# A selective state-space block beside a quantized feed-forward block on one core: six products of a step's second half go from VectorE to GpSimd, and the scan's result goes to SBUF

## The chip, the cores and the metric

The kernel runs on one core of one Trainium2 chip. The core has TensorE (PE in the profile, its weight loads PEld), VectorE (DVE), ScalarE (ACT), GpSimd (POOL) and SyncE (SP); each works through its own instructions in order, and here nearly all DMAs are issued from SP's queue. The metric is device time in microseconds for one launch. Before the change three runs took 5172.91, 5178.5 and 5181.34 us: the median is 5178.5 us.

## The reference

The input is x, 8 sequences of 1024 tokens with 512 channels. It is normalized over channels, and two blocks work on the result and are added to x:

```python
xn = _layernorm(x, axis=-1)
x = x + attn(xn) + ffn(xn)

# attn: D_INNER = 1024, D_STATE = 16
xz = xn @ W_in;  x_branch, z = split(xz, 2)
xc = silu(causal_depthwise_conv(x_branch, conv_w, 4 taps) + conv_b)
ssm = xc @ W_x;  B, C, dt = ssm[..., :16], ssm[..., 16:32], softplus(ssm[..., -1:] + dt_bias)
A = -exp(A_log)
h[t] = h[t-1] * exp(dt[t] * A) + (dt[t] * xc[t]) * B[t]     # per channel and state
y[t] = sum over states of h[t] * C[t]
out = ((y + xc * D_param) * silu(z)) @ W_out

# ffn: 512 -> 1408 -> 512; every operand is rounded blockwise to FP4 and back first
h = silu(q(xn) @ q(w_gate).T) * (q(xn) @ q(w_up).T)
out = q(h) @ q(w_down).T
```

The recurrence runs over 8 x 1024 tokens, 1024 channels and 16 states.

## The kernel before

**Steps and pairs.** The 8192 tokens are cut into 16 steps of T = 512, two steps to a sequence. A step's channels are 8 groups `j` of 128. The state-space part lays 32 channels times 4 states on the 128 partitions: a group `j` has 4 sets of 32 channels and 4 sets `q` of 4 states. Two sets of channels (`h` and `h + 1`) make one instruction of 2 x 512 columns, a *pair*. So a step has 8 x 4 x 2 = 64 pairs, numbered `k` = 0 to 63 in the order j, q, h, and the program 1024.

**What a pair does.** POOL makes `u` = (dt x) B (`make_u`, L638) in SBUF, from a pool with three buffers. ACT makes `ah` = exp(dt A) in PSUM, two instructions, two buffers (`make_a`, L650). In the second step of a sequence (odd steps) ACT also puts the carried state into one column of `u` (L656). In `scan`, DVE runs the recurrence over both halves in one instruction, `ah` times the running value plus `u`, and writes the states over `ah` (L668); in the first step of a sequence (even steps) it copies the last column into `state` (L673); then it multiplies the states by C into `hc` in SBUF (L675), from a pool with four buffers. PE sums over states with small matmuls (`sum_states`, L685) into `py`. After the last `q` of a group, DVE's `gate` (L703, L704) adds D x, multiplies by silu(z) and writes `y`, of which there is one buffer.

**Around the pairs.** `sweep` writes every engine's order out by hand. For pair g it issues `make_u` for pair g + 2, `make_a` for pair g + 1, then `scan` for pair g, then the work that `later` put off to this pair (`issue`), and then gives PE other work as long as a planned time per pair allows. That other work is, by place in the step: from pair 2 to 9 `finish`, the output matmul of the step before (`po`, L735); from pair 9 to 43 `ahead`, the projections for the next step (`px`, `pz`, L437 and L498), whose convolution runs on ACT and POOL (L454, L460); and in the rest the feed-forward matmuls. Steps 0 to 9 (SPLIT = 10) carry the gate and up matmuls with their quantization, which uses DVE, ACT and POOL; steps 10 to 15 carry the down matmul (`downs`, `pod`, L894), whose input `hTr` is loaded over SP's queue into two buffers (L883). DVE adds each result to the residual (`add`, L722). In step 15 there is no next step to project for.

**In a step's second half** `parameters` and `steps_of` prepare the next step. `parameters` is the matmul with W_x. `steps_of`, four times at a distance of three pairs, has ACT write softplus into two `dd` tiles (L577), then POOL multiply them by x (`rest`, L582) and SP store them (L584). There are two `dd` buffers, so ACT's next softplus waits until both stores have landed. SP's queue then holds the loads that follow in program order: `rep` (L593), B and C for the next step (L566), the gate's inputs (L696), `hTr` and the residual (L714).

Of the kernel before, what the change touches and what calls it, by code (L numbers as in the profile page):

```python
# [9 lines left out]
F32 = mybir.dt.float32  # L10
BF16 = mybir.dt.bfloat16
AF = mybir.ActivationFunctionType
ALU = mybir.AluOpType
# [4 lines left out]
P = 128  # L18
# [9 lines left out]
T = 512  # L28
SG = 4
D4 = P // SG  # L30
NQ = P // D4
NG = 4
FB = 256
SPLIT = 10
# [3 lines left out]
ENOUGH = 2.0  # L38
MOST = 6.0
AGAIN = "again"  # L40
TAIL = 12


# [134 lines left out]
class Net:  # L178
# [200 lines left out]
    def issue(self):  # L379
# [3 lines left out]
        while self.due.get(self.now):  # L383
            item = work, bank, key, act = self.due[self.now].pop(0)
            if key in [i[2] for i in kept] or (act and used >= ENOUGH and self.scanning):
                kept.append(item)
                continue
            if work() is AGAIN:
                kept.append(item)
# [103 lines left out]
    def project_z(self, s, j, w):  # L493
# [8 lines left out]
        def copy():  # L502
            if i == 0 and s.stored < h:
                return AGAIN
            if i == 0:
# [6 lines left out]
    def silus(self, s, h):  # L512
        nc = self.nc
        if s.convolved < 2 * (h + 1) or s.copied < 2 * (h + 1):
            return AGAIN
        xs, z = s.xc[:, 2 * h : 2 * h + 2, :], s.z[h]
# [117 lines left out]


    def make_u(self, s, j, q, h):
        u = self.pool.tile([P, 2, T], F32, tag="u", name=f"u_{s.c}_{j}_{q}_{h}", bufs=3)
        self.nc.gpsimd.tensor_tensor(  # L638
            u, s.reps[j][:, h : h + 2, 1, :], s.B[q].unsqueeze(1).to_broadcast([P, 2, T]), ALU.mult
        )  # L640
        self.us.append(u)
# [20 lines left out]
    def scan(self, s, j, q, h):  # L662

        nc = self.nc
        ah, u = self.ahs.pop(0), self.us.pop(0)
        g = j * NQ + h
        a = ah.rearrange("p i t -> p (i t)")
        nc.vector.tensor_tensor_scan(  # L668
            a, a, u.rearrange("p i t -> p (i t)"),
            0.0 if s.first else self.state[:, g, q : q + 1], ALU.mult, ALU.add,  # L670
        )
        if not s.last:
            nc.vector.tensor_copy(self.state[:, g : g + 2, q], ah[:, :, T - 1])  # L673
        hc = self.pool.tile([P, 2, T], F32, tag="hc", name=f"hc_{s.c}_{j}_{q}_{h}", bufs=4)
        nc.vector.tensor_tensor(hc, ah, s.C[q].unsqueeze(1).to_broadcast([P, 2, T]), ALU.mult)  # L675
        s.hcs.append(hc)

    def sum_states(self, s, j, q):

# [268 lines left out]
    def sweep(self, pairs, now, others, cost):  # L948
# [5 lines left out]
        left = cost + len(now) // per * (29.0 + 64.0 + sums)  # L954
        slots = len(now) - TAIL
        credit = 0.0
# [146 lines left out]
```

## Time and profile before

| | |
|---|---|
| median of three runs | 5178.5 us |
| the profiled execution | 5171.58 us, span 5169.7 us |
| mean granted TensorE clock | 0.916 |
| busy: PE, DVE, ACT, POOL | 4357.2, 4463.7, 3368.9, 4050.4 us (84, 86, 65, 78%) |
| steps 0 to 9 (460 to 3590 us): PE, DVE, POOL | 2720, 2688, 2603 of 3130 us |
| steps 10 to 14 (3591 to 4884 us) | 254 to 263 us a step |
| step 15 and the end | 286 us |

A profile line of the page's fifth part names line, engine and operation, then output<-inputs with shapes and the count; behind the bar stand the busy time in us, the mean of one in ns, and the engine's idle time just before these instructions with what ended it. In a table of stages each column is an engine's busy time in that stretch with its instruction count. A line of waits says who waited for whom, the total in us, how often, and the longest. The chain is followed back from the last instruction; a piece gives its start, its length and its work.

### The profile page before, as it was taken

Reading aid. Unit: us, or ns where it says so; the run is one execution under the profiler, and the core shown is the slowest. Engines: PE = TensorE matmul, PEld = TensorE weight load, DVE = VectorE, ACT = ScalarE, POOL = GpSimd, SP = SyncE. Lnnn points to the kernel's source line nnn. Section 1 sums busy time; section 2 is a strip of 40 time slices with the busy share of each in tenths; the row PEclk is TensorE's granted clock in tenths of the full one; section 3 lists DMA queues with packets and bytes.
Section 4 is the critical chain, followed back from the end, with each engine's and each line's share of the span. In section 5 each row is a group of like instructions: output and inputs, shape, how many; then the busy total and the mean of one; then the engine's idle time right before and its main releaser. Section 6 shows DMA issues by size and latency. Waiting matters only on the chain. (4 is left out here: it accounts for less than half of the span.)

```text
span 5169.7 us, 52154 instructions
## 1 busy us (share of the span) xinstructions
PE 4357.2 (84%) x16324; PEld 2286.0 (44%) x16324; DVE 4463.7 (86%) x4087; ACT 3368.9 (65%) x5037; POOL 4050.4 (78%) x2302
## 2 busy tenths in 40 slices
PE   5535889888898898989898898986999999999975
PEld 2324555554555556455554555551333333333321
DVE  6756888888888988888887898888999999999997
ACT  5655766767667677775767867676656665656543
POOL 5887888878888888887887888887768676767664
PEclk9656999999899999999999999996999999999986
DMA  6665566575656657566575656757686868686852
GB/s 196 198 205 157 143 185 182 155 199 170 180 165 173 192 165 208 143 188 180 162 201 154 191 166 182 200 145 207 178 229 177 239 182 240 175 236 184 228 132 61
DMA packets 582275, 937.45 MB, mean 181 GB/s; under 512 B 53216, under 2 KB 329696, under 8 KB 579824
## 3 DMA queue, kind: packets, MB, share of 16 engines
q1 hardware_dynamic: 571600, 931.61, 64.3%
q10 hardware_dynamic: 10400, 2.52, 0.2%
q8 instruction: 130, 2.13, 0.2%
q14 instruction: 145, 1.19, 0.1%
HBM read 676.76 MB, written 257.20 MB: 181 GB/s over the span
## 5 line engine op out<-in xcount | busy, mean ns | idle before, releaser
L638 POOL TENSOR_TENSOR u<-rep,B 128x1024 f32<-128x1024 f32 x1024 | 2411.3, 2361 | 760.9 <-DVE ah L668 691.6
L650 ACT ACTIVATE ah<-rep,A 128x512 f32<-128x512 f32 x2048 | 1415.8, 692 | 1129.0 <-DVE hc L675 1090.3
L675 DVE TENSOR_TENSOR hc<-ah,C 128x1024 f32<-128x1024 f32 x1024 | 1249.5, 1220 | 77.3 <-PE py L685 35.1
L668 DVE TENSOR_TENSOR_SCAN ah<-ah,state,u 128x1024 f32<-128x1024 f32 x512 | 1199.5, 2343 | 87.0 <-ACT u L656 85.9
L668 DVE TENSOR_TENSOR_SCAN ah<-ah,u 128x1024 f32<-128x1024 f32 x512 | 1169.3, 2284 | 52.3 <-ACT ah L650 46.0
L685 PE MATMUL py<-hc,summed 128*32 128x512 f32 x4096 | 653.5, 635 | 170.9 <-DVE hc L675 119.0
L771 PE MATMUL pu<-wu,xq 128*128 128x256 f32 (+1 forms) x3072 | 693.9, 383 | 101.9 <-ACT hT L824 63.1
L771 PE MATMUL pg<-wg,xq 128*128 128x256 f32 (+1 forms) x3072 | 661.7, 373 | 69.8 <-ACT hT L824 23.3
L771 PEld LDWEIGHTS pu<-wu,xq 128*128 128x128 f32 x3072 | 571.7, 203 | 250.6 <-ACT hT L824 86.7
L894 PE MATMUL pod<-dT,hTr 128*128 128x512 f32 x1408 | 641.7, 606 | 13.3 <-DMA hTr<-hT 9.6
L771 PEld LDWEIGHTS pg<-wg,xq 128*128 128x128 f32 x3072 | 554.0, 195 | 210.3 <-issue 69.5
L498 PE MATMUL pz<-xT,wz 128*128 128x512 f32 x1024 | 506.3, 641 | 69.5 <-ACT h L782 34.8
L437 PE MATMUL px<-xT,wx 128*128 128x512 f32 x1024 | 491.9, 625 | 38.8 <-ACT h L782 21.4
L735 PE MATMUL po<-Wout,y 128*128 128x512 f32 x1024 | 463.8, 604 | 10.7 <-ACT hT L824 4.4
L460 POOL TENSOR_TENSOR xc<-xc,taps 128x509 f32<-128x509 f32 x360 | 413.7, 1149 | 44.3 <-ACT taps L454 25.5
L894 PEld LDWEIGHTS pod<-dT,hTr 128*128 128x128 f32 x1408 | 262.7, 192 | 395.2 <-issue 365.1
L498 PEld LDWEIGHTS pz<-xT,wz 128*128 128x128 f32 x1024 | 204.1, 205 | 338.9 <-issue 232.3
L685 PEld LDWEIGHTS py<-hc,summed 128*32 128x32 f32 x4096 | 91.8, 110 | 564.7 <-DVE hc L675 278.7
L437 PEld LDWEIGHTS px<-xT,wx 128*128 128x128 f32 x1024 | 195.3, 198 | 317.7 <-issue 224.2
L735 PEld LDWEIGHTS po<-Wout,y 128*128 128x128 f32 x1024 | 191.2, 192 | 278.7 <-issue 258.4
L786 DVE TENSOR_TENSOR h<-h,pu 128x512 f32<-128x512 f32 x192 | 121.9, 638 | 179.4 <-PE pu L771 166.3
L650 ACT ACT_TABLE_LOAD x209 | 268.1, 1283 | 3.7
(125 smaller groups left out, 4538.4 us busy)
## 6 DMA issues: line engine op xcount, KB each, us to landing
rep<-ddd SPq DMA_DIRECT2D x512, 512.0 KB, 7.1
ddd<-dd SPq DMA_DIRECT2D x128, 512.0 KB, 3.5
hTr<-hT SPq DMA_DIRECT2D x64, 704.0 KB, 5.8
wg<-gu SPq DMA_DIRECT2D x80, 512.0 KB, 4.9
wu<-gu SPq DMA_DIRECT2D x80, 512.0 KB, 5.9
hT<-hT SPq DMA_DIRECT2D x80, 512.0 KB, 2.9
wx<-in_L_attn_W_in_dram SPq DMA_DIRECT2D x128, 256.0 KB, 3.0
wz<-in_L_attn_W_in_dram SPq DMA_DIRECT2D x128, 256.0 KB, 2.9
```

The lines of the kernel that those rows point to most:

```text
L437: nc.tensor.matmul(px, w[:, k, :], s.xT[:, k, :], start=(k == 0), stop=(k == self.KM - 1))
L460: tt(ca[:, H0 - k :], ca[:, H0 - k :], taps[k][:, : T - H0 + k], ALU.add)
L498: nc.tensor.matmul(b[0], w[:, k, :], s.xT[:, k, :], start=(k == 0), stop=(k == self.KM - 1))
L638: self.nc.gpsimd.tensor_tensor(u, s.reps[j][:, h : h + 2, 1, :], s.B[q].unsqueeze(1).to_broadcast([P, 2, T]), ALU.mult)
L650: nc.scalar.activation(ah[:, i, :], s.reps[j][:, h + i, 0, :], AF.Exp, scale=self.A[:, g, q : q + 1])
L668: nc.vector.tensor_tensor_scan(a, a, u.rearrange("p i t -> p (i t)"), 0.0 if s.first else self.state[:, g, q : q + 1], ALU.mult, ALU.add,)
L675: nc.vector.tensor_tensor(hc, ah, s.C[q].unsqueeze(1).to_broadcast([P, 2, T]), ALU.mult)
L685: nc.tensor.matmul(s.py[i * D4 : (i + 1) * D4, :], self.summed, hcs[i // 2][:, i % 2, :], start=(q == 0), stop=(q == NG - 1),)
L735: nc.tensor.matmul(b[0], s.y[:, j, i * P : (i + 1) * P], self.Wout[:, j, :], start=(j == 0), stop=(j == self.J - 1),)
L771: nc.tensor.matmul(b[0][:, i, :], xq[pair][:, k, i * P : (i + 1) * P], w[:, k, :], start=(k == 0), stop=(k == self.KM - 1),)
L786: nc.vector.tensor_tensor(rows, rows, b[0], ALU.mult)
L894: nc.tensor.matmul(b[0], h[:, k, :], dT[:, k, :], start=(k == 0), stop=(k == self.KF - 1))
```

## The change

For six pairs of every step from step 10 on, k = 42, 46, 50, 54, 58 and 62 (all with `h` = 0), the scan writes its states over `u` in SBUF instead of over `ah` in PSUM. For these pairs POOL instead of DVE copies the last column into `state` (even steps) and multiplies the states by C into `hc`. `ah` is then free when the scan ends, and the `u` buffer when POOL's product ends. The pool of `u` has four buffers instead of three, in all steps. POOL's new instructions stand in its queue where `scan` is issued, so behind `u` of pair k + 2 and ahead of what `issue` gives POOL at that pair and of `u` of pair k + 3.

```diff
+ASIDE = (42, 46, 50, 54, 58, 62)
...
     def make_u(self, s, j, q, h):
-        u = self.pool.tile([P, 2, T], F32, tag="u", name=f"u_{s.c}_{j}_{q}_{h}", bufs=3)
+        u = self.pool.tile([P, 2, T], F32, tag="u", name=f"u_{s.c}_{j}_{q}_{h}", bufs=4)
...
         a = ah.rearrange("p i t -> p (i t)")
+        uf = u.rearrange("p i t -> p (i t)")
+        aside = s.c >= SPLIT and (j * NG + q) * NQ // 2 + h // 2 in ASIDE
+        to = u if aside else ah
         nc.vector.tensor_tensor_scan(
-            a, a, u.rearrange("p i t -> p (i t)"),
+            uf if aside else a, a, uf,
             0.0 if s.first else self.state[:, g, q : q + 1], ALU.mult, ALU.add,
         )
+        hc = self.pool.tile([P, 2, T], F32, tag="hc", name=f"hc_{s.c}_{j}_{q}_{h}", bufs=4)
+        s.hcs.append(hc)
+        C = s.C[q].unsqueeze(1).to_broadcast([P, 2, T])
+        if aside:
+            if not s.last:
+                nc.gpsimd.tensor_copy(self.state[:, g : g + 2, q], to[:, :, T - 1])
+            nc.gpsimd.tensor_tensor(hc, to, C, ALU.mult)
+            return
         if not s.last:
-            nc.vector.tensor_copy(self.state[:, g : g + 2, q], ah[:, :, T - 1])
-        hc = self.pool.tile([P, 2, T], F32, tag="hc", name=f"hc_{s.c}_{j}_{q}_{h}", bufs=4)
-        nc.vector.tensor_tensor(hc, ah, s.C[q].unsqueeze(1).to_broadcast([P, 2, T]), ALU.mult)
-        s.hcs.append(hc)
+            nc.vector.tensor_copy(self.state[:, g : g + 2, q], to[:, :, T - 1])
+        nc.vector.tensor_tensor(hc, to, C, ALU.mult)
```

## The prediction

> **What bounds the kernel now.** I read the profiled execution in this order: the shares of the chain that ended last, busy time by stage, who waits for whom in the stages that are edited, and the chain piece by piece there. From the page, the chain's shares and two groups:
>
> ```profile
> DVE ah L668 11%; DVE hc L675 5%; PE po L735 4%; PE pod L894 3%; ACT ah L650 1%; PE py L685 1%; DMA xz<-z 1%; PE pz L498 0%; DMA hTr<-hT 0%; DMA rep<-ddd 0%; POOL u L638 0%; PE pu L771 0%; DVE py L703 0%; DVE r_True L722 0%; ACT taps L454 0%
> ...
> L638 POOL TENSOR_TENSOR u<-rep,B 128x1024 f32<-128x1024 f32 x1024 | 2411.3, 2361 | 760.9 <-DVE ah L668 691.6
> ...
> L675 DVE TENSOR_TENSOR hc<-ah,C 128x1024 f32<-128x1024 f32 x1024 | 1249.5, 1220 | 77.3 <-PE py L685 35.1
> ```
>
> The operation that moves, `hc`, costs 1.22 us on DVE; POOL's nearest row, `u`, with the same shapes and kinds of operand, costs 2.36 us. POOL idles 692 us before its `u`, waiting for a scan to give a buffer back. The chain is DVE, but with PE in it. Busy time by stage, for the first 42 pairs and the rest of steps 14 and 15 (columns: PE, weight loads, DVE, ACT, POOL, granted clock, DMA):
>
> ```profile
> 4629.90:4798.70 168.80, 163.56 (x470) 60.81 (x471) 160.88 (x148) 100.48 (x147) 128.25 (x75) 0.98 0.71 192
> 4798.70:4884.00 85.30, 83.89 (x253) 30.44 (x251) 83.88 (x78) 46.69 (x66) 60.48 (x30) 1.00 0.90 253
> 4884.00:5053.90 169.90, 131.30 (x368) 42.64 (x366) 161.64 (x109) 75.18 (x143) 100.22 (x43) 0.84 0.57 143
> 5053.90:5134.00 80.10, 38.46 (x92) 3.90 (x92) 78.27 (x48) 35.37 (x68) 44.67 (x19) 0.50 0.25 59
> ```
>
> In the second half of step 14, the edited part, DVE and PE are both busy 98% at a granted clock of 1.00. In step 15 the down matmul is over and PE is half idle: there DVE alone sets the time. So what PE waits for matters in steps 10 to 14. PE's waits in the second halves of step 10 (two lines) and of step 14:
>
> ```profile
> PE pod L894 <- DMA hTr<-hT: 4.1, 2, 3.2
> PE py L685 <- DVE hc L675: 0.8, 1, 0.8
> ...
> PE py L685 <- DVE hc L675: 1.4, 1, 1.4
> ```
>
> Steps 11, 12 and 13 have 1.9, 2.0 and 1.5 us. All five together are 4.9 + 1.9 + 2.0 + 1.5 + 1.4 = 11.7 us, and PE can be shortened there by no more. At the start of the next step DVE waits for PE (start of step 15; steps 11 to 14 show the second line with 0.7 to 0.8 us):
>
> ```profile
> DVE r_True L722 <- PE po L735: 3.8, 3, 3.4
> DVE y L704 <- PE po L735: 0.7, 1, 0.7
> ```
>
> `y` has one buffer, so the first gate of a step, about pair 9, waits until PE has finished the step before. A lead that DVE gains and PE does not is given back there. The chain in step 14 shows two more links:
>
> ```profile
> 4834.22 1.28 POOL dd L582
> ...
> 4835.52 8.01 DMA ddd<-dd
> ...
> 4843.60 1.21 ACT L577
> ...
> 4849.06 2.31 DVE ah L668
> ...
> 4852.73 1.05 PE py L685 x4
> 4853.79 9.64 PE pod L894 x22
> ```
>
> POOL's `dd` product is stored; the store must land before ACT may write the next `dd`; ACT stands before the next `ah`, and DVE waits for that. From 4852.73 on, PE runs without a gap into step 15.
>
> **The change, part by part.**
>
> *Removed from DVE.* 36 `hc` (six steps, six pairs) and 18 state copies (the even steps). The copy, 0.16 us, overlaps the end of the scan and the start of `hc`, so what goes is the distance between two scans. In step 15, around pairs 51 to 53:
>
> ```profile
> 5087.38 2.35 DVE L668 TENSOR_TENSOR_SCAN ah<-ah,state,u 128x1024 f32<-128x1024 f32 x1
> 5089.76 1.23 DVE L675 TENSOR_TENSOR hc<-ah,C 128x1024 f32<-128x1024 f32 x1
> 5090.90 2.35 DVE L668 TENSOR_TENSOR_SCAN ah<-ah,state,u 128x1024 f32<-128x1024 f32 x1
> ```
>
> From start to start it is 3.52 us, of which 2.35 is scan: about 1.17 us saved a pair, 36 x 1.17 = 42 us if nothing else held.
>
> *The scan that writes SBUF.* No scan does so in this trace. The nearest rows of 512 columns (L786 0.64, L704 0.69 into SBUF, L703 0.75 into PSUM) differ by 0.11 us, so the bound is plus or minus 0.11 x 36 = 4 us; I take 0, as the recurrence, not the destination, sets 2.29 us for 1024 columns against 1.22 of a plain product.
>
> *Added to POOL.* 36 products of 2.36 us (bounds 2.36 by `u`, 2.54 by two `dd` of 1.27) and 18 copies of about 0.19 (L464): 88 us, 14 to 15 in a half where POOL has 25 us idle. Each new product waits for its scan, and behind it stand the `u` three pairs on (2.5 + 2.4 = 4.9 us after the scan's end, wanted 7.1 after: covered) and the `dd` products, then SP's stores of `dd` and all loads queued on SP behind them. The order of PE, ACT and SP is unchanged.
>
> A rule that speaks against such a move: the Trainium skill, Trace Analysis, section on optimizing Scalar and DVE operations, says that POOL and DVE share an SBUF read port, so that shifting work between them may not help. The row against it: `hc` with one input in PSUM, one in SBUF and its output in SBUF, which the edited scan will be like, takes 1.214 to 1.227 us 1024 times, whatever POOL runs. By the rule the sum would lose what I price below; by the row it loses 0.
>
> *Step 15.* ACT has the next `ah` ready 0.5 us before the scan ends, `u` over 4 us, and PE waits. Six pairs of 1.17: -7.0 us, all on the path.
>
> *Steps 10 to 14*, by the time at which PE's last stretch begins:
> - Step 10: POOL runs the second pair of `dd` behind the product of pair 50, not before it. They ended at 3799.4; now scan 50 ends about 3797.7 (1.75 earlier), then 0.2 + 2.4 + 2.5 gives 3802.8, 3.4 later. SP's `hTr` load behind that store was issued at 3801.2 and PE waited 3.2 us for it; it goes 3.4 later, and 0.4 to 0.9 of the later `hTr` wait absorbs a part: +3.0.
> - Step 11: PE's 1.9 us wait for the gate at pair 58. DVE comes there with 1.17 of pair 42, little of 46 (ACT's softplus makes the next `ah` late), part of 50: -1.75.
> - Step 12: both waits for `hc`, 1.3 us, go and part of the `hTr` wait of 0.7: -1.7.
> - Step 13: the wait of 1.5 us goes if the store of the third `dd` pair lands in the usual 3.7 us (-1.5); it took over 8, and POOL issues it about 0.7 later (+0.7). Middle: -0.4.
> - Step 14: POOL's `dd` of the chain above ends at scan 50's end + 0.2 + 2.4 + 2.4 + 2.5. That scan ends 2.4 earlier, but a product and a copy more stand ahead of it: 0.1 later than before. With the same 8 us of landing nothing is gained; with 3.7, 1.4. I take -0.6.
>
> Sum -1.5 us; the bounds are -11.7 (all PE waits gone) and +12 (3 in four of the five).
>
> *The fourth `u` buffer* serves all sixteen steps. It lets POOL start one pair earlier where it now waits for a scan, 292 us in steps 0 to 9. But what other engines wait for POOL there, and POOL itself could have begun after such a wait, is small: DVE waited for `u` 3.9 us in all, ACT 11.7, PE's transposes for the last quantizing product 33, most of them with POOL busy up to that point. Bounds 0 and -18; I take -2.5.
>
> **Sum.** -7.0 - 1.5 - 2.5 = -11.0 us. The profiled execution took 5171.6 us (span 5169.7 and 1.9 around it), 6.9 below the median of the three runs, 5178.5; by it 5160.6, by the median 5167.5.
>
> **Rivals.**
> 1. *DVE alone is the bound* (for: its shares; against: 98% PE and its 11.7 us of waits). All 42 us come: 5136.
> 2. *Slower: the `dd` stores hold SP.* If in every step the second pair of `dd` falls behind a product as in step 10, `hTr` loads come 3.4 us late, and the softplus after them too. For: SP waited 32 us for `dd` products around the second half of step 10, and DMA is at 0.90. Against: in steps 11 to 14 `hTr` is mostly issued 9 to 14 us before use and lands in about 5.8. It decides once a `dd` ends over 4 us late: 5 x 3.4 = 17, less 7: 5188.5.
> 3. *The buffer is worth its upper bound* of 18: 7.0 + 1.5 + 18 = 26.5, 5152. For: POOL's 292 us; against: nobody waits long for it.
> 4. *POOL and DVE block each other.* Half a POOL product, 1.2 us, per edited scan is 43, less 11: 5210. Only the rule speaks for it.
> 5. *The change does nothing*: with PE bound to the end, 5178. Step 15, with PE half idle, speaks against it.
>
> **How the numbers follow.** The forecast has 0.60, and its own range, from its bounds, is 5157 to 5178; half of that lies beyond 0.2% (10.4 us, about what a measurement of this kernel can tell from no change), half within. Rival 1 has 0.06, 2 has 0.18, 3 has 0.12, 4 has 0.02, 5 has 0.02. Faster: 0.30 + 0.06 + 0.12 = 0.48; same: 0.30 + 0.02 = 0.32; slower: 0.18 + 0.02 = 0.20. Leaving out rival 1 and part of 3 below, and 4 and part of 2 above, gives 5150 to 5187.
>
> **What would show it.** Right: scans at the edited pairs of step 15 start 2.4 us after the one before and its second half is 7 us shorter; PE's waits in the second halves of steps 11 and 12 vanish and step 10's wait for `hTr` grows to over 6; DVE's wait for `po` at pairs 3 to 9 grows by what DVE gained. Wrong: second halves of steps 10 to 14 that are 5 us shorter without longer waits at the next step's start (rival 1), PE waits for `hTr` in every step (2), steps 0 to 9 shorter by over 10 us (3), or edited scans over 2.5 us (4).

## The result: 0.2% faster, and the profile after

Twenty runs of each kernel beside one another: 5163.82 us after (5153.99 to 5180.17), 5175.34 before (5161.43 to 5188.0). The ratio is 0.998, with a 95% interval of 0.9972 to 0.9988: 10.4 us faster (6 to 14.5). The predicted sum was 11.0.

The profiled execution has a span of 5171.4 us, longer than the 5169.7 of before. Its steps 0 to 9, where only a buffer was added, happen to end 12.2 us later (step 10 starts at 3603.1, before at 3590.9); steps 10 to 15, where the work moved, take 1568.3 us instead of 1578.8. Executions of one kernel spread over 26 us, so single profiles are read here only by stage, and a stretch of five steps is not known better than to some 7 us (e1 below, whose time is that of before, has 1282.5 us where before has 1289.9).

From the page after the change, the shares of the chain and the group of `u`:

```profile
PE pod L904 7%; DVE ah L672 6%; PE po L745 4%; DVE hc L686 3%; PE py L695 2%; ACT ah L651 1%; DMA xz<-z 1%; DMA hTr<-hT 1%; PE pz L499 1%; PE ps L538 1%; DMA rep<-ddd 1%; POOL u L639 1%; PE px L438 1%; POOL xc L461 1%; PE pu L781 0%
...
L639 POOL TENSOR_TENSOR u<-rep,B 128x1024 f32<-128x1024 f32 x1024 | 2402.2, 2362 | 380.4 <-DVE ah L672 262.1
```

The down matmul, 3% of the chain before, leads it now; the scan went from 11% to 6%. POOL's wait for a scan to give a `u` buffer back fell from 692 to 262 us. The instructions on `u` (count, then shortest, median and longest in ns):

```profile
L672 DVE TENSOR_TENSOR_SCAN ah<-ah,u x494: 2233/2289/2299, 463.6 to 4886.7; 128x1024 f32<-128x1024 f32 x165
L672 DVE TENSOR_TENSOR_SCAN ah<-ah,state,u x494: 2257/2350/2359, 795.5 to 5132.9; 128x1024 f32<-128x1024 f32 x165
L682 POOL TENSOR_TENSOR hc<-u,C x36: 2338/2354/2391, 3781.4 to 5133.1; 128x1024 f32<-128x1024 f32 x36
L672 DVE TENSOR_TENSOR_SCAN u<-ah,u x18: 2278/2278/2283, 3778.9 to 4883.4; 128x1024 f32<-128x1024 f32 x18
L681 POOL COPY state<-u x18: 186/188/194, 3781.3 to 4885.8; 128x2 f32<-128x2 f32 x18
L672 DVE TENSOR_TENSOR_SCAN u<-ah,state,u x18: 2340/2340/2345, 4045.5 to 5130.7; 128x1024 f32<-128x1024 f32 x18
```

The edited scans take 10 ns less than the others, and POOL's product 2.35 us. The busy times by stage, for both parts of steps 14 and 15 (columns: PE, weight loads, DVE, ACT, POOL, granted clock, DMA):

```profile
4640.10:4807.30 167.20, 162.05 (x473) 60.46 (x472) 160.98 (x149) 100.62 (x147) 130.49 (x76) 0.99 0.73 197
4807.30:4890.20 82.90, 80.55 (x243) 29.14 (x242) 76.09 (x66) 46.63 (x66) 73.13 (x41) 1.00 0.88 245
4890.20:5063.00 172.80, 133.94 (x377) 43.63 (x375) 161.70 (x109) 75.16 (x143) 101.57 (x44) 0.84 0.58 148
5063.00:5171.40 108.40, 64.23 (x160) 16.68 (x160) 76.26 (x49) 35.26 (x68) 57.91 (x25) 0.64 0.22 58
```

The second half of step 14 was 85.3 us with VectorE busy for 83.88; now it is 82.9 with 76.09. VectorE has lost 7.8 us of work and the stage 2.4. The second half of step 15 with the end of the program went from 115.8 to 108.4, where VectorE lost 7.5: everything arrived. This is the list of VectorE's instructions around pair 51 of step 15 (start, duration):

```profile
5090.34 2.34 DVE L672 TENSOR_TENSOR_SCAN u<-ah,state,u 128x1024 f32<-128x1024 f32 x1
5092.60 2.33 DVE L672 TENSOR_TENSOR_SCAN ah<-ah,state,u 128x1024 f32<-128x1024 f32 x1
5094.96 1.23 DVE L686 TENSOR_TENSOR hc<-ah,C 128x1024 f32<-128x1024 f32 x1
```

From the edited scan to the next it is 2.26 us; with a product between it is 3.50 here and was 3.52 before. An edited pair saves 1.26 us, not the 1.17 of the prediction: the next scan begins 0.08 us before the recorded end of this one.

Measured from pair 10 of a step (behind the point where VectorE waits for the end of the step before) to pair 10 of the next, in us:

| | step 10 | 11 | 12 | 13 | 14 | sum 10 to 14 | step 15 to the end |
|---|---|---|---|---|---|---|---|
| before | 260.3 | 259.3 | 255.1 | 260.1 | 255.1 | 1289.9 | 238.8 |
| after | 264.5 | 254.6 | 256.4 | 255.6 | 255.3 | 1286.2 | 231.7 |

In these five steps 30 x 1.26 = 38 us of VectorE's time went, and 3.6 of it came out (the sums are made of unrounded starts); traces of one kernel can differ by more than that here. The first table of waits shows who holds VectorE in this stretch, first before, then after the change (total us, times, longest):

```profile
DVE ah L668 <- ACT u L656: 12.1, 13, 2.8
DVE r_True L722 <- PE po L735: 11.6, 13, 3.4
DVE ah L668 <- ACT ah L650: 11.1, 4, 4.9
DVE r_False L722 <- DMA r_False<-in_L_attn_x_dram: 7.0, 2, 6.4
DVE y L704 <- PE po L735: 3.8, 5, 0.8
DVE r_True L722 <- DMA r_True<-rd: 1.9, 1, 1.9
```

```profile
DVE ah L672 <- ACT u L657: 20.2, 16, 3.3
DVE r_False L732 <- DMA r_False<-in_L_attn_x_dram: 13.7, 4, 7.6
DVE ah L672 <- ACT ah L651: 11.7, 4, 5.1
DVE r_True L732 <- DMA r_True<-rd: 11.3, 6, 5.6
DVE ah L672 <- POOL dd L583: 10.2, 2, 5.8
DVE r_True L732 <- PE po L745: 7.3, 10, 4.2
DVE r_False L732 <- DMA C<-ssm_d: 3.9, 1, 3.9
```

The prediction had VectorE's lead given back to PE (`po`). That wait fell from 11.6 to 7.3. What grew is the wait for residuals that `add` needs (7.0 + 1.9 before, 13.7 + 11.3 after, and the 3.9 of the last line, which is an `add` too) and the wait for a late `ah` or for the column of `u` that ACT fills. The line that names POOL's `dd` belongs there too: in step 14 that `dd` had ended 12 us before the scan, and ACT's `ah` came last. All lines of the scan together went from 23.2 to 42.1 us.

### The profile page after: what moved, and what is told of

Its sections match the earlier page's. It is cut to its first block, busy times and chain, and to the rows that moved or that the text cites. A ratio compares the mean times of both kernels' runs of the same rounds, so it can differ in the third digit from the quotient of the medians.

```text
span 5171.4 us, 52167 instructions
## 1 busy us (share of the span) xinstructions
PE 4348.0 (84%) x16324; PEld 2285.1 (44%) x16324; DVE 4419.0 (85%) x4033; ACT 3369.1 (65%) x5037; POOL 4127.5 (80%) x2356
## 5 line engine op out<-in xcount | busy, mean ns | idle before, releaser
L686 DVE TENSOR_TENSOR hc<-ah,C 128x1024 f32<-128x1024 f32 x988 | 1205.5, 1220 | 81.1 <-PE py L695 39.2
L672 DVE TENSOR_TENSOR_SCAN ah<-ah,state,u 128x1024 f32<-128x1024 f32 x494 | 1157.0, 2342 | 98.9 <-ACT u L657 97.8
L672 DVE TENSOR_TENSOR_SCAN ah<-ah,u 128x1024 f32<-128x1024 f32 x494 | 1128.1, 2284 | 65.7 <-ACT ah L651 50.3
L695 PE MATMUL py<-hc,summed 128*32 128x512 f32 x4096 | 638.8, 632 | 164.8 <-DVE hc L686 96.7
L814 POOL TENSOR_TENSOR h<-h,rs 128x1024 f32<-128x1024 f32 x96 | 171.8, 1790 | 175.1 <-DVE rs L810 149.2
L816 POOL TENSOR_TENSOR h<-h,qm 128x1024 f32<-128x1024 f32 x96 | 189.0, 1969 | 124.0 <-ACT qm L63 120.1
```

The source lines that it names most:

```text
L672: nc.vector.tensor_tensor_scan(uf if aside else a, a, uf, 0.0 if s.first else self.state[:, g, q : q + 1], ALU.mult, ALU.add,)
L686: nc.vector.tensor_tensor(hc, to, C, ALU.mult)
L695: nc.tensor.matmul(s.py[i * D4 : (i + 1) * D4, :], self.summed, hcs[i // 2][:, i % 2, :], start=(q == 0), stop=(q == NG - 1),)
L816: self.later(3, lambda: tt(v, v, m[0], ALU.add), key="g")
```

## The experiments

Two theories stood at the start. *PE*: PE is full in steps 10 to 14, and takes back what VectorE gains. *The loads and the softplus*: POOL's products push the `dd` products back, behind them SP's stores and the loads queued there, and ACT's softplus. All ratios are to the kernel before, run beside each.

| run | what it is | median, us | ratio [95%] | sum 10 to 14, us | step 15, us |
|---|---|---|---|---|---|
| e1_buffer | fourth `u` buffer alone | 5176.08 | 1.0004 [0.9994, 1.0015] | 1282.5 | 238.9 |
| e2_last | pairs of step 15 alone | 5165.74 | 0.9981 [0.9971, 0.9991] | 1292.0 | 230.7 |
| e3_not10 | pairs of steps 11 to 15 | 5167.69 | 0.9983 [0.9972, 0.9993] | 1287.2 | 231.8 |
| e4_behind | POOL's product behind `dd` | 5165.32 | 0.9981 [0.9973, 0.9990] | 1287.6 | 231.1 |
| e5_light_before | before, 5 of 11 down matmuls left out | 5138.63 | 0.9941 [0.9928, 0.9955] | 1266.9 | 238.8 |
| e6_light_after | after, 5 of 11 left out | 5139.21 | 0.9942 [0.9928, 0.9955] | 1270.5 | 230.4 |
| e8_fourth | step 15 alone, every fourth pair | 5147.88 | 0.9959 [0.9947, 0.9972] | 1289.1 | 219.6 |
| e10_firsthalf | the same, and first halves of 10 to 14 | 5149.35 | 0.9965 [0.9952, 0.9979] | 1284.1 | 220.8 |
| e11_rest | after, residuals loaded earlier | 5162.00 | 0.9982 [0.9973, 0.9991] | 1291.7 | 230.5 |
| e12_rest_before | before, residuals loaded earlier | 5169.05 | 1.0002 [0.9991, 1.0014] | 1292.2 | 239.5 |
| e13_both | e11 and a third `dd` buffer | 5151.79 | 0.9965 [0.9954, 0.9976] | 1280.8 | 231.0 |
| e14_both_before | e12 and a third `dd` buffer | 5166.31 | 0.9995 [0.9986, 1.0004] | 1289.9 | 238.9 |

### The buffer and the last step alone: e1_buffer, e2_last

e1 is the kernel before with the buffer only:

```diff
-        u = self.pool.tile([P, 2, T], F32, tag="u", name=f"u_{s.c}_{j}_{q}_{h}", bufs=3)
+        u = self.pool.tile([P, 2, T], F32, tag="u", name=f"u_{s.c}_{j}_{q}_{h}", bufs=4)
```

> The kernel before with the fourth u buffer alone, no pair set aside. My theory: the buffer is worth little, because hardly anybody waits for POOL: whole time 0 to 5 us below before, steps 10 to 15 (from the first scan of step 10 to the end) within 2 us of before's 1578.8, POOL's wait for a scan before its u down by about half. Rival, the buffer carries the whole gain: ratio 0.998, about 11 us, most of it in steps 0 to 9.

e2 is the changed kernel with its pairs in step 15 only:

```diff
-        aside = s.c >= SPLIT and (j * NG + q) * NQ // 2 + h // 2 in ASIDE
+        aside = s.c == self.n - 1 and (j * NG + q) * NQ // 2 + h // 2 in ASIDE
```

> The changed kernel with the six pairs set aside in step 15 alone; the fourth u buffer stays. My theory: the second half of step 15 is 7.4 us shorter, as in the changed kernel (115.8 to 108.4), and steps 10 to 14 stay at before's lengths: steps 10 to 15 take 1571 to 1572, whole time 7 to 10 us below before. Rival, every product is worth the same 10.5 / 36 = 0.29 us wherever it is: 1.8 us, not to be told from no change.

The buffer takes POOL's wait for a scan from 692 to 363 us (page of e1) and the time stays, 1.0004:

```profile
L638 POOL TENSOR_TENSOR u<-rep,B 128x1024 f32<-128x1024 f32 x1024 | 2404.6, 2361 | 484.3 <-DVE ah L668 363.4
```

POOL makes `u` earlier, and hardly anybody had waited for it. Six products in step 15 give 0.9981, as much as all 36 (0.998). So the other 30 products of the change are worth nothing that can be measured here, where each interval reaches some 5 us to either side.

### Step 10 left out, and POOL's order turned round: e3_not10, e4_behind

e3 tests the prediction's term for step 10 (3 us lost, since `dd` falls behind a product):

```diff
-        aside = s.c >= SPLIT and (j * NG + q) * NQ // 2 + h // 2 in ASIDE
+        aside = s.c > SPLIT and (j * NG + q) * NQ // 2 + h // 2 in ASIDE
```

> The changed kernel without the six pairs of step 10; steps 11 to 15 as changed. My theory: step 10 loses by the change, because the second pair of dd products stands behind the product of pair 50 and SP's hTr load behind their store. Without it the second half of step 10 goes from 89.1 back to about 85.3, PE's wait for hTr there from 7.2 to about 4.1, and steps 10 to 15 take 1564 against 1568.3. Rival, DVE alone is the bound and step 10 gained as the others did: 6 x 1.17 = 7 us more, 1575.

e4 keeps all pairs, and issues POOL's copy and product behind the work that `issue` gives POOL at that pair, the `dd` products among it:

```diff
-            if not s.last:
-                nc.gpsimd.tensor_copy(self.state[:, g : g + 2, q], to[:, :, T - 1])
-            nc.gpsimd.tensor_tensor(hc, to, C, ALU.mult)
+            def product():
+                if not s.last:
+                    nc.gpsimd.tensor_copy(self.state[:, g : g + 2, q], to[:, :, T - 1])
+                nc.gpsimd.tensor_tensor(hc, to, C, ALU.mult)
+
+            self.put_off.append(product)
...
             self.issue()
+            while self.put_off:
+                self.put_off.pop()()
```

> The changed kernel with POOL's copy and product of a pair set aside placed behind what is issued at that pair, so that the dd products of the same pair come first; nothing else moves. My theory: step 10's dd pair no longer waits for scan 50, its second half goes to 83 to 86 and steps 10 to 15 to 1562 to 1566. Rival, the sums on PE wait for the later hc instead (2.5 us later where a dd pair now stands ahead): second halves of steps 10, 11 and 13 up to 2.5 us longer, 1568 to 1576.

PE's waits in the second half of step 10, in the changed kernel and then in e3:

```profile
PE pod L904 <- DMA hTr<-hT: 7.2, 3, 5.2
```

```profile
PE pod L904 <- DMA hTr<-hT: 3.9, 1, 3.9
PE py L695 <- DVE hc L686: 0.8, 1, 0.8
```

The size of the term for step 10 holds, and the products of step 10 cause it. With the change SP issues that `hTr` load 38.5 us after pair 42 instead of 34.9 (3.6 later; 3.4 predicted), PE waits 7.2 instead of 4.1, and the half is 89.1 us; in e3 it is 85.3 again, as before. But steps 10 to 15 took 1570.6 us in e3 and 1568.9 in e4, 3 to 7 us more than I expected of either, and the time did not move. What e3 gained in step 10, step 13's first half lost in its trace (181.0 instead of 177.6).

e4 shows that the late load is not all of it. Its second pair of `dd` products in step 10 and the `hTr` load behind their store are 0.7 and 1.0 us earlier than before the change. Yet the second half of step 10 takes 88.3 us, not the 83 to 86 that I expected, and PE still waits 7.1 us for `hTr`: at pair 53 3.7 instead of the 5.2 of the changed kernel (3.2 before), but at pair 62 3.1 (1.6 and 0.9). A load that SP issues 4.6 us earlier than in the changed kernel, at 33.8 instead of 38.5 us after pair 42, lets PE go on only 1.6 us earlier. The second halves of steps 11, 12 and 14 fall to 80.3, 80.0 and 81.5 us in e4, and then the next steps' first halves are longer. In step 10 VectorE, too, still waits 4.2 us for a residual at pair 53, and 5.5 at pair 62. In the kernel before the `add` at pair 53 starts 46.2 us after pair 42, behind a wait of 0.6 us; in e4 at 46.6, behind one of 4.2. The residual comes when it came before the change; VectorE, whose scan 53 starts 3.3 us earlier (38.75 instead of 42.01 after pair 42), waits for it. So a lead of VectorE ends at this `add`, whose residual used to come just in time.

### PE made light: e5_light_before, e6_light_after

Both leave out five of the eleven matmuls of each down product, so that PE has room in every step. e5 is the kernel before, e6 the changed one.

```diff
             for k in range(self.KF):
-                nc.tensor.matmul(
-                    b[0], h[:, k, :], dT[:, k, :], start=(k == 0), stop=(k == self.KF - 1)
-                )
+                if k % 2 == 0:
+                    nc.tensor.matmul(
+                        b[0], h[:, k, :], dT[:, k, :], start=(k == 0), stop=(k == self.KF - 1)
+                    )
```

> The kernel before, with 5 of the 11 matmuls of every down tile left out (the odd blocks of 128 inner channels are not summed), so that PE has slack in steps 10 to 14; all orders stay. My theory: PE holds the start of each step, so DVE's waits for po at pairs 3 to 9 shrink or go, and steps 10 to 14 are 3 to 8 us shorter each than before's. Rival, PE does not bind: steps 10 to 14 keep their 254 to 263 us.

> The changed kernel with the same 5 of 11 down matmuls left out. Compared with the lightened kernel before it: my theory, with PE out of the way the DVE time saved in steps 11 to 14 comes through except for what the dd products, their stores and ACT's softplus take: 3 to 6 us a step from one pair 10 to the next, 12 to 24 us for steps 11 to 14, where the full kernels differed by 7.5 (4.7 - 1.3 + 4.5 - 0.2). Step 10 still gains less than the others or loses, by the loads behind the dd stores. Rival, POOL, SP and ACT hold it and PE is not the cause: the same 5 to 9 us for the four steps together, with or without the matmuls.

If PE alone took the gain back, the change would bring up to 38 us in steps 10 to 14 here. It brings nothing: 1266.9 us without it, 1270.5 with it. In steps 11 to 14 alone it brings 2.4 us, less than the 12 to 24 that I expected and than the rival's 5 to 9. The whole times, of four runs each, are alike as well (5138.63 and 5139.21 us), although step 15 is 8.4 us shorter in the trace of e6. VectorE's waits in these steps, in e5 and then in e6:

```profile
DVE ah L668 <- ACT u L656: 12.7, 15, 2.4
DVE ah L668 <- ACT ah L650: 5.2, 3, 4.5
DVE r_False L722 <- DMA r_False<-in_L_attn_x_dram: 4.8, 1, 4.8
DVE r_True L722 <- PE po L735: 1.5, 3, 1.1
```

```profile
DVE ah L672 <- ACT u L657: 21.2, 18, 3.3
DVE r_False L732 <- DMA r_False<-in_L_attn_x_dram: 19.8, 4, 7.7
DVE r_True L732 <- DMA r_True<-rd: 12.0, 6, 8.8
DVE ah L672 <- POOL dd L583: 6.2, 1, 6.2
DVE ah L672 <- ACT ah L651: 4.6, 2, 3.9
```

The wait for `po` is gone, residuals take 32 us instead of 4.8, and a late `ah` 36 instead of 18. PE is not the only holder: this theory, the prediction's own, fell as the sole cause. (That PE binds too shows in e5 itself: the same steps are 23 us shorter than in the kernel before.)

### Where the products pay, and more of them: e8_fourth, e10_firsthalf

If only step 15 gains, it can have more pairs. e8 sets every fourth pair from 10 to 62 aside, in step 15 alone; e10 adds five pairs in the first halves of steps 10 to 14, where the `dd` products are not yet due.

```diff
-ASIDE = (42, 46, 50, 54, 58, 62)
+ASIDE = range(10, 63, 4)
...
-        aside = s.c >= SPLIT and (j * NG + q) * NQ // 2 + h // 2 in ASIDE
+        aside = s.c == self.n - 1 and (j * NG + q) * NQ // 2 + h // 2 in ASIDE
```

> Pairs are set aside in step 15 alone, but every fourth one from pair 10 to 62: 14 instead of 6. My theory: where PE is half idle each pair set aside gives 1.25 us, so step 15 takes 14 x 1.25 = 17.5 us less than before's (285.6 to 268), 10 less than with six pairs in step 15 alone (0.9981); ratio 0.9962. POOL needs 4 x 2.36 + 2.4 = 11.9 us for four pairs, DVE 13.0. Rival, POOL or PE's rest of the down tiles at pairs 12 to 25 holds the first half: 8 us, not 17.5, ratio 0.998.

```diff
+EARLY = (12, 18, 24, 30, 36)
...
+        aside = s.c >= SPLIT and (j * NG + q) * NQ // 2 + h // 2 in (ASIDE if s.c == self.n - 1 else EARLY)
```

> As the kernel with every fourth pair of step 15, and pairs 12, 18, 24, 30 and 36 of steps 10 to 14 set aside as well; none in their second halves. My theory: PE waits for DVE 5 to 8 us in each of these first halves, so half of the 5 x 1.25 us comes through: 2 to 4 us a step, 10 to 20 us beyond the kernel with step 15 alone; ratio 0.993 to 0.995. Rival, what DVE gains in a first half is given back at the next step's start as in the second halves: nothing beyond that kernel, 0.996 to 0.997.

Step 15 in e8, first 42 pairs and the rest (columns as above):

```profile
4880.50:5039.70 159.20, 124.95 (x368) 42.84 (x366) 151.50 (x100) 74.90 (x143) 115.22 (x50) 0.88 0.61 152
5039.70:5146.90 107.20, 60.88 (x160) 16.21 (x160) 76.31 (x49) 35.40 (x68) 57.91 (x25) 0.69 0.21 59
```

From pair 10 to the end it is 219.6 us instead of 238.8: 19.2 us for 14 products, 1.37 each. That is at least the whole 1.26 of each; where the rest comes from stays open, and single traces differ by 1 to 2 us in such a stretch. The time is 0.9959, 5147.88 us: the lowest ratio of the versions that compute the whole result, with 14 products moved instead of 36 (e13's 0.9965, below, lies inside its interval). The 25 products that e10 adds in earlier steps bring nothing that can be measured (0.9965, where I had expected 0.993 to 0.995).

### Residuals earlier, and a third dd buffer: e11_rest to e14_both_before

Four runs together, with and without the change. In e11 and e12 the residual of a down product is loaded one tile ahead, with three buffers, and the first residual of the output matmul at pair 50 of its own step. e13 and e14 add a third buffer for `dd` (and for the taps that share it), with three `u` buffers in both.

```diff
         def load(t):
...
             hs.append(h)
+            rs.append(self.rest(fp, t))
...
-            r = self.rest(fp, t)
+            r = rs.pop(0)
...
+            if k == 50 and c >= SPLIT and c * self.TT in self.r_seen:
+                s.r0 = self.rest(self.pool, c * self.TT)
...
-        rs = [self.rest(self.pool, s.c * self.TT)]
+        rs = [s.r0 or self.rest(self.pool, s.c * self.TT)]
```

```diff
-            dd = self.pool.tile([P, 2, T], F32, tag="dd", name=f"dd_{c}_{j}")
+            dd = self.pool.tile([P, 2, T], F32, tag="dd", name=f"dd_{c}_{j}", bufs=3)
```

> The changed kernel, with the residual loads of steps 10 to 15 issued earlier: the down matmul's residual r is loaded one tile ahead, beside the next hTr and with three buffers instead of two, and the first residual of the output matmul is loaded at pair 50 of the step itself instead of pair 0 of the next. Theory (what VectorE gains in steps 10 to 14 is lost to residuals that land late): VectorE's waits for r loads of 12.9 + 3.9 us in step 10, 6.9 in step 12, 1.6 and 2.1 in 11 and 14 go, and at least half of these 27 us stays: steps 10 to 14, from pair 10 of step 10 to pair 10 of step 15, take 1286 us in the changed kernel and 1268 to 1276 here, and the time is 0.994 to 0.996 of the kernel before. Rival (the loads are late but another wait, ah, hTr or PE, ends at the same moment): 1281 to 1289 us, ratio 0.997 to 0.999.

> The control: the kernel before, with the same earlier residual loads. Its VectorE waits for r loads only 7.0 us in step 10 and 1.9 in step 12. Theory: 1282 to 1288 us from pair 10 of step 10 to pair 10 of step 15 (1290 in the kernel before), ratio 0.998 to 1.000, so the run with the change gains at least 8 us more in these steps than this one. Rival: the same 1282 to 1290, and the two differ by less than 5.

> The changed kernel with the earlier residual loads and, beside them, three buffers for dd instead of two (and three for u, to make room; the fourth was worth nothing). The softplus of a second dd tile then waits for the store of a tile further back. Theory (the dd products that come later on POOL hold ACT's softplus, and so ah at pairs 55 and 56): the waits for ah of 4.4 and 5.8 us at pair 55 of steps 12 and 14 and of 3.3 at pair 56 of steps 11 and 13 shrink by half or more, and pair 10 of step 10 to pair 10 of step 15 is 5 to 9 us shorter than with the earlier residual loads alone: 1260 to 1270, ratio 0.993 to 0.995. Rival (PE takes the time back in the next step's start, where VectorE waits for po): within 3 us of the run with the earlier residuals alone.

> The control: the kernel before with the earlier residual loads and three dd buffers. Its waits for ah at pairs 55 and 56 are 0.6 us at most but one of 1.5, so both theories give the time of the control without the third buffer, within 3 us; the difference between the two runs with both edits, with and without the change, is what POOL's products are worth once these waits are gone: 20 us or more by the theory (42 us at most), 11 or less by the rival.

e11 is a miss for the theory. The waits for residual loads are all gone, and the time stays at 0.9982. VectorE's longest waits in e11:

```profile
DVE ah L672 <- ACT u L657: 24.6, 18, 5.0
DVE r_True L732 <- PE po L745: 21.8, 15, 6.2
DVE ah L672 <- ACT ah L651: 11.7, 4, 5.4
DVE ah L672 <- POOL dd L583: 9.0, 2, 4.7
DVE r_False L732 <- PE pod L905: 5.7, 4, 1.7
DVE hc L686 <- PE py L695: 4.1, 3, 2.1
```

The wait for `po` rose from 7.3 us in the changed kernel to 21.8, but most of that is not the change's doing. Its control e12, where no product is moved, has almost the same:

```profile
DVE r_True L722 <- PE po L735: 20.2, 15, 6.0
DVE ah L668 <- ACT u L656: 13.7, 15, 2.8
DVE ah L668 <- ACT ah L650: 11.2, 3, 4.9
```

With the residuals out of the way, `po` is the next in line at almost the same moment, in both kernels. What the change adds is read from the difference of the two: VectorE is busy 1185.4 us instead of 1222.5 in these steps and idle 36.6 more. Of these, 25.0 are waits for a late `ah` or `u` (24.9 in e12, 49.9 in e11), 1.6 for `po`, and 12 for PE's down products and sums (the lines of `pod` and `py`, 1.4 in e12). So e6 and e11 complement each other: with little work on PE the residuals hold, without the residuals PE's down products and sums. A late `ah` holds in both, and in every pair of runs it grew with the change: from 23.2 to 42.1 us in the full kernels, 17.9 to 35.7 from e5 to e6, 24.9 to 49.9 from e12 to e11, 23.7 to 37.9 from e14 to e13.

The late `ah` is the link that the prediction had followed in step 14. These are POOL's, then ACT's instructions there in the changed kernel (start, duration, and in brackets the idle time before and what ended it):

```profile
4837.88 2.35 POOL L682 TENSOR_TENSOR hc<-u,C 128x1024 f32<-128x1024 f32 x1
4840.19 2.37 POOL L639 TENSOR_TENSOR u<-rep,B 128x1024 f32<-128x1024 f32 x1
4842.50 2.51 POOL L583 TENSOR_TENSOR dd<-dd,xc 128x512 f32<-128x512 f32 x2
```

```profile
4852.01 1.28 ACT L578 ACT_TABLE_LOAD   x1 [5.24 <-DMA ddd<-dd]
4853.30 1.34 ACT L578 ACTIVATE dd<-row,dtb 128x512 f32<-128x512 f32 x2
4854.65 1.28 ACT L651 ACT_TABLE_LOAD   x1
4855.95 1.41 ACT L651 ACTIVATE ah<-rep,A 128x512 f32<-128x512 f32 x2
```

`dd` ends at 4845.0, ACT waits until the stores have landed, 7.0 us later, then softplus, the table for exp and `ah`, and the scan of pair 55 starts at 4857.45. Counted from pair 42 of the step (4807.27) that is 50.2 us; before the change it was 4849.06 less 4798.71, 50.3. The products of pairs 42, 46 and 50 are moved, VectorE is 4.0 us ahead at pair 54 (42.1 instead of 46.1), and at pair 55 it is where it had been.

With the third `dd` buffer pair 55 of step 14 starts 48.1 us after pair 42. The waits for `ah` and `u` at pairs 55 and 56 of steps 11 to 14 are 10.8 us together, in e11 18.3 and in the changed kernel 16.9: less, but not by the half that I expected. The time goes from 0.9982 to 0.9965 (9 us; the two intervals just overlap); the control goes from 1.0002 to 0.9995. Between e13 and e14 the change is worth 0.0030 of the time, 15.5 us (give or take some 7, from the two intervals), between e11 and e12 0.0020, 10. In the traces step 15 gives 8.0 us of e13's gain and steps 10 to 14 give 9.1 (1289.9 to 1280.8); in e11 these are 9.0 and 0.5. So 15.5 lies between the 20 us or more that I expected and the rival's 11 or less, and decides between them no more than the spread of 7 us allows.

What is left holds on ACT and on PE. Against its control e14, VectorE in e13 still waits 14.2 us longer for `ah` and `u`, 14.4 longer for PE's down products and sums, and only 2.2 longer for `po` (22.1 and 19.9). In the second halves of steps 11 and 13 PE is busy 99% (79.68 of 80.20 us and 81.58 of 81.80). In steps 10, 12 and 14 PE itself waits 8.6, 2.3 and 1.7 us for `hTr` (4.1, 1.3 and none in e14), so that loads hold there as well. A version with all holders taken away (PE's load, the residuals, the softplus) was not run, so that they are all is not shown.

## Why the prediction was right, and where its steps were not

**The sum, -11.0: met, in part by luck.** The gain is that of step 15 (7.1 us in the traces, 7.0 predicted; e2, with the pairs of step 15 alone, has 0.9981). The other two terms, -1.5 and -2.5, are smaller than what was measured can tell from nothing, and the waits they were worked out from did not behave as forecast. The range, 5157 to 5178, doesn't follow from the bounds of the terms either: added up, they give 5142 to 5184.

**Step 15, -7.0: right, and slightly too small.** The second half with the end is 7.4 us shorter; e2 has as much as the whole change from it. The saving is 1.26 us a pair rather than 1.17, because a scan follows a scan with no gap.

**The scan into SBUF, 0: right.** 2278 against 2289 ns, 2340 against 2350.

**POOL's added work: right in size.** 2.35 us a product, 0.19 a copy; the second half of step 14 has 12.7 us more on POOL, now 73 of 82.9.

**Step 10, +3.0: right in size, the link only in part.** SP's issue of `hTr` is 3.6 us later, the second half 3.8 longer, and e3 undoes both. But in e4 the load goes out earlier than before the change and the half is still 3.0 us longer: residuals hold VectorE there, and PE waits for `hTr` at pair 62.

**Steps 11 to 14, -4.5 together by PE's waits: the sum fits, the steps do not.** From pair 10 to pair 10 these four steps are 7.8 us shorter, which is as much as such a stretch differs between traces. But the waits that were to vanish in steps 11 and 12 did not: step 11 still has 1.5 us for the gate and 0.3 for `hTr`, step 12 1.5 for `hc` and 2.5 for `hTr`. The step that failed is "DVE comes there with 1.17 of pair 42, little of 46 (...), part of 50". I had a late `ah` behind pair 46 in it, which costs 1.0 us, but followed the chain from POOL's `dd` over the store and the softplus to the late `ah` of pair 55 in step 14 only, where it came out almost as computed (`dd` ends 0.1 us later by the prediction, 0.3 earlier by the trace). It runs in all of steps 11 to 14: `ah` is late at pair 55 in step 12 as well (4.4 us), at pair 56 in steps 11 and 13 (3.3 us). In e13, where that hold is shorter, PE's waits in steps 11 and 13 do go, from 1.8 each to 0.5 and 0.2. That of step 12 for `hTr` stays (2.3).

**Who takes the lead back: wrong in the main.** I named `po`, and said that VectorE's wait for it would grow by what VectorE gained. It fell from 11.6 to 7.3, because residual loads, which I had looked at only as something queued behind `dd`, and a late `ah` held VectorE first. The trace of before already showed such a load: VectorE waited 6.4 us for a residual at the start of step 11, where I had read only the wait for `po`. With the residuals loaded early `po` is long with and without the change (21.8 in e11, 20.2 in e12), so it takes back 1.6 us of about 37. The forecast that little comes of steps 10 to 14 was right for another reason than the one given.

**The buffer, -2.5: too much.** e1 has 1.0004; zero fits it, and 2.5 us is just inside the interval's edge (0.9994, 3 us). My lower bound was the value.

**The rivals.** 1 (all 42 us) fell: 30 of 36 products brought next to nothing. 2 (`hTr` late in every step) happened in step 10 only: the other second halves are 2.2 to 3.0 us shorter, though PE's wait for `hTr` grew in step 12 (0.7 to 2.5) and step 14 (none to 1.0). 3 (the buffer worth 18) fell with e1. 5 (nothing) lies outside the interval. 4 (POOL and VectorE block each other): beside 88 us more of POOL, VectorE's `hc` has the same median (1224 ns) in both kernels and the edited scans are shorter than the rest. The rule of the Trainium skill, Trace Analysis, section on optimizing Scalar and DVE operations, that such a shift may not help, doesn't show here for products and scans that have one operand in PSUM and one in SBUF; in step 15 every moved product paid in full.

## What to carry to other kernels

Work taken off the busiest engine pays where that engine alone sets the end, here the last step, where six products brought as much as thirty-six, and fourteen brought twice that. Where another engine is nearly full and loads land just in time, list everything that the relieved engine meets next, loads for its own side work too, and ask of each how much slack it has: here, taking away one holder (e6, e11) let the others hold at nearly the same moment. Compare each wait with that of a control that has the same edits without the change; a long wait that the control has too is not what took the gain. Before moving work to a helper engine, follow what stands behind it in that engine's queue, through store, reuse of the buffer and next producer, in every repetition of the stage and not in one.

## What was not expected of the hardware

A product starts 0.03 to 0.11 us behind the recorded end of the scan whose states it reads, and a scan that waits for nothing starts 0.08 to 0.09 us ahead of the recorded end of the product, the `add` or the scan before it. So removing the product between two scans saves 1.26 us although it lasts 1.23. A scan that writes its states over an SBUF input is 10 ns shorter than one that writes them over PSUM (2278 and 2340 ns against 2289 and 2350).
